# Cross scores in two steps with a shared bias product, and a planned order with a pause before each buffer's next use and longer weight loads

## The chip, the cores and the metric

The kernel runs on one core of one Trainium2 chip, in one launch. The metric is the device time of one execution in microseconds (us), from the runs listed below; smaller is better. TensorE (PE in the profile, its weight loads PEld), VectorE (DVE), ScalarE (ACT), GpSimd (POOL) and SyncE (SP, which here issues all DMAs) each work through their own queue of instructions in the order in which the program holds them, and wait for each other by semaphores.

## The reference

A decoder block with three sublayers, each followed by a residual sum and a layer norm, on x of shape (4, 512, 128) in fp32.

```python
def attn(x, Wq, Wk, Wv, Wg, Wa, ba, Wo, gn_w, gn_b):         # 16 heads of 64
    q, k, v = silu(x @ Wq), silu(x @ Wk), x @ Wv
    cum = cumsum(-softplus(x @ Wa + ba))
    decay = exp(where(causal, cum[i] - cum[j], -inf))
    o = ((q @ k.T) * decay) @ v
    o = groupnorm_over_tokens_and_channels_of_a_head(o) * gn_w + gn_b
    return (o * sigmoid(x @ Wg)) @ Wo

def xattn(ctx, query, W1, b1, W2, b2, W3):                    # 32 keys per sample
    q, k = query @ W1.T + b1, ctx @ W2.T + b2
    return (softmax(q @ k.T / 32) @ ctx) @ W3.T

def ffn(x, ...):                                              # 6 layers
    for i in range(6):
        # 16 heads of 64, windows of 32 tokens that also see the window before
        q, k, v = split(shift_tokens(x) @ Wqkv[i])
        q, k = rotary(l2norm(q) * q_scale[i]), rotary(l2norm(k) * k_scale[i])
        x = softmax(mask(q @ k.T * 8)) @ v @ Wo[i] + x
        a, gate = split(layernorm(shift_tokens(x)) * g + b @ W1[i] + b1[i])
        x = (a * gelu(gate)) @ W2[i] + b2[i] + x
    return x

x = layernorm(x + attn(x, ...))
x = layernorm(x + xattn(ctx, x, ...))
x = layernorm(x + ffn(x, ...))
```

## The kernel before

**Stages.** The front (class `Front`) does the first attention sample by sample, eight pairs of heads for each (`pair`), then the norm (`finish`) and the cross attention (`cross`). The layers (class `Layers`) work in units: layer, sample, half of the heads, token tile, 6 x 4 x 2 x 4 = 192 units. A unit projects q and k (three fp32r products each, lines 87 to 89, the `pq` and `pk` tiles), squares and rotates them (ACT line 1258, DVE lines 1242 and 1251, POOL line 1264), scales them by the inverse norm (POOL line 1362), transposes both (line 96, `ptq` and `ptk`), makes the window scores `s` (lines 1408 and 1421, 72 products on 64x32 tiles of the array, called S in the plan), the softmax (DVE 1441 and 1450, ACT 1460 and 1463, DVE 1466 and 1467, POOL 1473), transposes the result (line 1483, `pp`, then ACT 1487) and multiplies it by the values into `O` (line 1499, 64 products on 128x32 tiles). The values of two tiles are projected together and moved into window order by eight pairs of DMAs (`vb<-v`, lines 1313 to 1325). After the two halves of a sample its attention is added (`add_attention`), and the feed-forward part follows (`ffn`).

**Cross scores.** `cross` folds W1, W2 and the biases into a matrix M and a row br (made once in `setup_b`). For each sample it multiplies four token tiles by M (128 rows in the array) and adds br by a product with one row in the array, tile after tile, in one planned step:

```python
for t in range(NT):
    nc.tensor.matmul(view()[:, t, :], lhsT=x[:, tslice(t)], rhs=M[:, keys], start=True, stop=False)
    nc.tensor.matmul(view()[:, t, :], lhsT=unit, rhs=br[:, keys], start=False, stop=True)
```

An fp32 product of this kind is two passes, hence x2 for each in the profile.

**What sets the order.** Nothing is issued as it is written. Each step is recorded by `do` with its engine, a cost, what it reads and writes, and a priority: the number of its unit or pair plus an offset from the table `SHIFT`, by the step's name (group letter and running number). `Plan.order` then plays the steps through in the plan's own clock and writes down the order in which they start; that order is the program, on every engine. In it an engine takes the ready step of lowest priority number. On TensorE it may take another one whose priority is up to `KEEP` larger, if a change of kind costs less: `TURNS` and `TURN` hold what the plan charges for a change between kinds (`t` transposes, `S`, `O`, `f` the last product of the feed-forward part, `None` the projections). A step that writes a buffer starts only if one of that sort is free (`ROOM`: 3 + 2 + 2 + 1 banks of PSUM, 2 raw buffers for weights, and so on), and a buffer is counted free at the moment when its last user's planned cost has passed. `LAG` is what lies between a step's end and the start of another that needs it, `DMA` the same for loads of weights. The figures in these tables are the plan's own, not measurements.

**Loads of weights.** `load_half` and `load_values` load through the two raw buffers: `w0` and `w3` are the loads of Wq and Wk (lines 1067), `w6` of Wo (line 1086), `w7` of Wv (line 1089, tiles `wv00r` for layer 0 and half 0, `wv01r` for half 1), whose transposes `wvt` and products `wvo` (line 1100) fold Wv with Wo. `load_ffn` loads W1 (`w1r`, line 1157) and folds the bias (`pb`, line 1162). All are issued by SP, in the planned order, and the first layer's wait for the last sample's fifth pair of heads.

Of the kernel before, what the change touches and what calls it, by code (L numbers as in the profile page):

```python
# [20 lines left out]
B, S, D = 4, 512, 128  # L21
NT = S // P
H, DH = 16, 64
SK = 32
# [10 lines left out]
def tslice(t):  # L35
    return slice(t * P, (t + 1) * P)
# [97 lines left out]
class Plan:  # L134
# [5 lines left out]

    LAG = 0.25

    TURN = 0.04
    TURNS = {
# [3 lines left out]
    }  # L148

    KEEP = 4.5  # L150

    def __init__(self, room):
        self.room, self.steps, self.last = dict(room), [], {}
# [26 lines left out]
    def order(self):  # L180
        free, left, need, ready, after = dict(self.room), {}, {}, {}, {}
# [13 lines left out]
        waiting, busy, out, events, kinds = {}, set(), [], [], {}  # L195
# [24 lines left out]
        now = 0.0  # L220
        while events:
            now = events[0][0]
            while events and events[0][0] <= now + 1e-9:
                _, _, over, st = heapq.heappop(events)
                if not over:
                    heapq.heappush(waiting.setdefault(st.eng, []), (st.prio, st.n, st))
                    continue
                busy.discard(st.eng)
                for s in st.slots:
                    left[s] -= 1  # L230
                    if left[s] == 0 and s.tags:
                        free[s.got] += 1
            for eng, q in waiting.items():
                if eng in busy:
                    continue
                passed, pick, best = [], None, 0.0
                while q:
                    it = heapq.heappop(q)
                    if pick is not None and it[0] > least + self.KEEP:
                        passed.append(it)  # L240
                        break
                    took = room(it[2])
                    if took is None:
                        passed.append(it)
                        continue
                    give(took)
                    turn = self.turn(eng, kinds.get(eng), it[2].kind)
                    if pick is None:
                        least = it[0]
                    elif turn >= best:  # L250
                        passed.append(it)
                        continue
                    else:
                        passed.append(pick)
                    pick, best = it, turn
                    if turn == 0.0:
                        break
                for it in passed:
                    heapq.heappush(q, it)
                if pick is None:  # L260
                    continue
                st = pick[2]
                took = room(st)
                for s, g in took.items():
                    s.got = g
                busy.add(eng)
                st.start = now
                out.append(st)
                cost = st.cost + best
                kinds[eng] = st.kind  # L270
                heapq.heappush(events, (now + cost, st.n, 1, st))
                for nx, d in after.get(st, ()):
                    need[nx] -= 1
                    ready[nx] = max(ready[nx], now if d is None else now + cost + d)
                    if need[nx] == 0:
                        heapq.heappush(events, (ready[nx], nx.n, 0, nx))
# [5 lines left out]
class Work:  # L282
# [5 lines left out]
        t1=8, t2=4, sq=2, nx=2, n2=3, r=4, u=2, v=2, qT=2, kT=3, pr=3, mx=3, su=3, pT=2, vb=2,  # L288
# [3 lines left out]
    )  # L292

    SHIFT = dict(
        C1=5.5, C2=8.5, C3=-2.75, D0=19.5, D2=12.75, D3=-11.25, D4=-0.5, D6=3.25, D7=12.25, D8=-1.25, D9=-7.75,
        D10=-7.25, I0=-0.5, I2=1.25, N0=1, N1=21.5, N2=0.5, N3=-14.75, N4=-22, N5=-27, N6=5.25, O0=-0.25,
        O1=-17.25, O2=-10.5, O4=-0.25, P0=-3.75, P1=14.25, P2=19.75, P3=-2.75, P4=13, P5=8.5, P8=-9.5, P9=-3.5,
        P10=-1, P11=125.75, P12=-12.5, P13=-2.25, P14=4, P15=4.5, P16=-4.5, P17=0.25, P18=42.75, P19=-0.25,
        P20=11.5, P21=40.5, P22=-0.75, P23=-26.75, P24=-1.25, P25=-0.25, P26=-3, P27=-0.75, P28=-7.5, P29=-0.75,
        P30=0.25, P31=18.5, P32=52.25, P33=-1.5, P34=3.75, P35=-24, P36=11.5, P37=-8.25, P38=7.75, P39=6, S0=-2,  # L300
        S1=18.25, S2=18, S3=24.75, S4=4.75, S5=3, S7=33.5, S8=-2, V0=-0.25, V1=48.5, V2=-82.5, V3=-19, V4=-27.25,
        V5=-11, V6=1.5, V7=19.25, W0=13.5, W1=-1.5, W2=-4, W3=21, W4=-4.5, W5=-2, W6=2, W7=-6.25, W8=-0.25,
        W9=-0.25, W10=4, W11=0.75, X1=28.25, X2=-0.5, X3=-1.75, X4=-2, X5=42.25, X6=3.25, X7=1.25, X8=127.5,
        X9=24.75, X10=-7.25, X11=0.25, X12=-0.5, X13=-6.75, X14=-4.75, X15=-11, X16=4.5, X17=-0.5, a0=-0.25,
        a1=-0.25, a2=4.25, a3=4.25, f0=-22.25, f1=-1.75, f2=54.25, f3=-5, f4=-30, f5=-5.5, f6=-5, f7=-9.25,
        f8=-26.25, f9=7.5, f10=1, f11=0.25, f12=-37.5, f13=-6.75, f14=-13.75, f15=-6.5, f16=0.5, f17=-46.5,
        f18=4.25, f19=-14.75, f20=8, f21=3.25, f22=-30.25, f23=8.5, f24=-6.5, f25=-39.75, f26=81.5, f27=5.25,
        f28=-61.75, f29=12.5, g0=-15.5, g1=1.25, g2=5.75, g3=0.75, g4=-1.5, g5=7.25, g6=-1.75, k0=-1.75, k2=-1.5,
        k3=12, k4=2, k5=-16, k6=17.5, k7=2, p0=33.5, p1=10.25, q0=2.25, q1=-2.25, q2=-10.25, q3=-4.75, q4=-0.25,
        q5=1.75, q6=0.75, q7=-16.25, q8=-23, q9=-9, q10=-2.75, q11=-6.75, q12=-1.25, q13=-22.5, t0=7.25,  # L310
        t1=-31.75, t2=-1, t3=-3.25, t4=-29, t5=-6.75, t6=6.75, u1=7.25, u2=2.25, u3=2.25, u4=-20.75, u6=-1.5,
        u7=2.25, u8=3.25, u9=-12.25, u10=-7.25, u11=40.25, u12=31.25, u13=-2, u14=-1.75, u15=-23.75, u16=9,
        u17=0.5, u18=-7.75, u19=1.25, u20=9.5, u21=34.75, u23=-12, u24=-59.75, u25=-14.5, u26=-23, u27=-53.5,
        u28=-45.5, u29=-49.75, u30=-29, u31=-36.25, u32=-58, v0=6.75, v1=-0.5, v2=2, v4=0.5, v5=5.25, v6=-2.75,
        w0=-19, w1=2, w2=-4, w3=-58.25, w4=35.5, w5=-17.75, w6=-3, w7=2.75, w8=3.25, w9=-1, w10=1.5, w11=-10,
        w12=-6, w13=-4.75, w14=2.5, w15=-1.75,
    )

    PE3, PE_T, PE_S, PE_AV = 0.73, 0.37, 0.72, 1.01
    SPD = 0.62  # L320
    A512, V512 = 0.49, 0.61
    G_ADD, G_MUL, G16 = 1.25, 1.01, 0.23
    DMA = 8.0

    def __init__(self, k, plan):
        self.k, self.plan = k, plan
# [1 line left out]
    def do(self, eng, cost, fn, r=(), w=(), off=0.0, **kw):  # L328
        name = f"{self.group}{self.count}"
        self.count += 1  # L330
        self.plan.step(eng, cost, fn, r, w, prio=self.base + off + self.SHIFT.get(name, 0.0), **kw).name = name
# [73 lines left out]
class Front(Work):  # L405
# [571 lines left out]
    def cross(self, b):  # L977
        k, nc, do = self.k, self.k.nc, self.do
        M, br, cw, unit = self.bw
# [4 lines left out]
        pq = self.bank("mm", "pq" + nm)  # L984
        view = lambda: pq()[:, 0 : NT * SK].rearrange("p (t k) -> p t k", t=NT)

        def scores():
            for t in range(NT):
                nc.tensor.matmul(view()[:, t, :], lhsT=x[:, tslice(t)], rhs=M[:, keys], start=True, stop=False)
                nc.tensor.matmul(view()[:, t, :], lhsT=unit, rhs=br[:, keys], start=False, stop=True)  # L990

        do("PE", 2.7, scores, [X, bs], [pq], kind="g")
        sm = self.slot("bs", [P, 2, NT], "bs" + nm)
        e = self.slot("be", [P, NT, SK], "e" + nm)
        wide = lambda j: sm()[:, j].unsqueeze(2).to_broadcast([P, NT, SK])
# [36 lines left out]
class Layers(Work):  # L1032
# [47 lines left out]
    def load_values(self, W, l, h2):  # L1080
# [13 lines left out]
        for e in range(2):  # L1094
            rows = slice(e * 64, e * 64 + 64)
            ps = self.bank("mm", f"wvo{nm}{e}")

            def prod(ps=ps, rows=rows):
                for p in range(4):
                    nc.tensor.matmul(  # L1100
                        ps()[:, tslice(p)], lhsT=wt()[rows, tslice(p)], rhs=wo()[rows, p, :], start=True, stop=True
                    )

            self.do("PE", 0.85, prod, [wt, wo], [ps])
            self.do("ACT", self.A512, lambda ps=ps, e=e: nc.scalar.copy(hi()[:, e], ps()), [ps], [hi])
            self.do(
                "DVE",
                self.V512,
                lambda ps=ps, e=e: nc.vector.tensor_tensor(out=lo()[:, e], in0=ps(), in1=hi()[:, e], op=ALU.subtract),
                [ps, hi],  # L1110
                [lo],
            )
# [708 lines left out]
```

## Time and profile before

| | us |
|---|---|
| median of 3 runs | 2003.3 (2001.99 to 2007.96) |
| profiled execution, device time | 2008.77 |
| its span, first to last instruction | 2007.1 |
| busy: TensorE | 1850.5 (92%) |
| busy: VectorE | 1611.1 (80%) |
| busy: ScalarE | 1587.4 (79%) |
| busy: GpSimd | 1441.8 (72%) |
| mean granted TensorE clock | 0.976 of full |

The busy time is the union of an engine's instructions in one profiled execution. Matmuls are pipelined, so that the length of one product is more than it adds; what a group of products adds is read from the end of the group before to its own end. Idle time is put down to what ended it; "issue" means that nothing that the profile shows was waited for. The slices of the page are 50.2 us each. The front fills the first 360 us or so, then six layers of about 260 us each, which overlap at their borders.

### The profile page before, as it was taken

How to read it: one execution, taken by the hardware profiler on the slowest of the kernel's cores; microseconds unless marked ns; L12 is line 12 of the kernel's file. 1: busy time of each engine (PE TensorE's matmuls, PEld its weight loads, DVE VectorE, ACT ScalarE, POOL GpSimd, SP SyncE). 2: the span in 40 equal slices, each digit the busy share in tenths (PEclk: the TensorE clock that was granted, in tenths of full speed). 3: DMA queues.
4: the chain of work that ended last, by engine and by line, in shares of the span. 5: the costliest groups of instructions: out<-in, count | busy, mean ns of one | idle time of the engine just before them, and what ended most of it. 6: DMA issues, size and time to landing. Idle time of an engine off the chain costs nothing.

```text
span 2007.1 us, 71083 instructions
## 1 busy us (share of the span) xinstructions
PE 1850.5 (92%) x28633; PEld 1405.3 (70%) x28633; DVE 1611.1 (80%) x3482; ACT 1587.4 (79%) x4048; POOL 1441.8 (72%) x1847
## 2 busy tenths in 40 slices
PE   7999999788898999989999999999999998999996
PEld 5676677566676777767777777777777776767675
DVE  5787786757787798886998868989788897888885
ACT  7877765689887788878888888888878897788785
POOL 3444444666777688886887878878878888787882
PEclk9999997789999999999999999999999999999999
DMA  3000001254555565665555555656655565545662
GB/s 90 1 6 2 1 2 34 67 130 109 133 148 123 131 152 139 156 150 147 133 132 146 146 146 142 166 123 160 150 142 144 125 157 149 142 107 134 146 172 60
DMA packets 146464, 233.02 MB, mean 116 GB/s; under 512 B 23770, under 2 KB 39000, under 8 KB 146136
## 3 DMA queue, kind: packets, MB, share of 16 engines
q1 hardware_dynamic: 146136, 228.46, 45.7%
q8 instruction: 228, 3.74, 0.8%
q14 instruction: 100, 0.82, 0.1%
HBM read 31.25 MB, written 2.10 MB: 17 GB/s over the span
## 4 chain that ended last, share of the span: by engine, by line
PE 57%; ACT 18%; DVE 14%; DMA 4%; issue 3%; SPq 3%; POOL 1%; DVEq 0%; ACTq 0%; POOLq 0%
PE O L1499 6%; PE s L1421 4%; PE pv L87 4%; DMA vb<-v 4%; PE pv L89 3%; PE pv L88 3%; PE ptk L96 3%; PE pp L1483 3%; PE ptq L96 2%; SPq L1325 2%; PE pyf L1625 2%; DVE nx L1275 2%; ACT sq L1258 2%; ACT v L1306 2%; PE pq L87 1%
## 5 line engine op out<-in xcount | busy, mean ns | idle before, releaser
L1264 POOL TENSOR_TENSOR t1q<-t1q,t2q 128x512 f32<-128x512 f32 x192 | 248.7, 1295 | 66.4 <-DVE t2q L1251 62.6
L1264 POOL TENSOR_TENSOR t1k<-t1k,t2k 128x512 f32<-128x512 f32 x192 | 251.3, 1310 | 55.4 <-DVE t2k L1251 40.7
L1473 POOL TENSOR_TENSOR pr<-pr,su 128x512 f32<-128x512 f32 x192 | 204.2, 1068 | 91.0 <-DVE su L1467 73.7
L1306 ACT COPY v<-pv 128x512 f32<-128x512 f32 x384 | 219.8, 602 | 42.7 <-PE pv L89 37.4
L1275 DVE TENSOR_REDUCE nx<-sq 128x16 f32<-128x1024 f32 x192 | 231.8, 1207 | 4.9 <-ACT sq L1258 3.7
L1499 PE MATMUL O<-vb,pT 128*32 128x128 f32 x6144 | 210.9, 279 | 10.5 <-DMA vb<-v 4.8
L1499 PEld LDWEIGHTS O<-vb,pT 128*32 128x32 f32 x6144 | 165.0, 111 | 63.3 <-issue 30.3
L1362 POOL TENSOR_TENSOR t1q<-t1q,r 128x512 f32<-128x512 f32 x192 | 201.2, 1051 | 2.7
L1362 POOL TENSOR_TENSOR t1k<-t1k,r 128x512 f32<-128x512 f32 x192 | 200.9, 1049 | 0.0
L1421 PE MATMUL s<-kT,qT 64*32 64x64 f32 x12288 | 169.8, 223 | 22.6 <-issue 22.5
L1460 ACT ACTIVATE pr<-s,mx 128x64 f32<-128x64 f32 x768 | 178.2, 325 | 9.8 <-DVE mx L1441 9.8
L1441 DVE TENSOR_REDUCE mx<-s 128x4 f32<-128x256 f32 x384 | 145.6, 413 | 42.7 <-PE s L1421 41.3
L1242 DVE TENSOR_TENSOR t1k<-pk,tl 128x512 f32<-128x512 f32 x192 | 130.7, 681 | 56.0 <-PE pk L89 34.8
L1242 DVE TENSOR_TENSOR t1q<-pq,tl 128x512 f32<-128x512 f32 x192 | 130.7, 681 | 50.7 <-PE pq L89 37.0
L1421 PEld LDWEIGHTS s<-kT,qT 64*32 64x32 f32 x12288 | 151.0, 105 | 25.0 <-issue 24.5
L1258 ACT ACTIVATE sq<-pk 128x512 f32<-128x512 f32 x192 | 116.1, 610 | 41.6 <-DVE t1k L1242 23.9
L1251 DVE TENSOR_TENSOR t2q<-pq,tl 128x512 f32<-128x512 f32 x192 | 130.0, 677 | 21.0 <-ACT sq L1258 20.1
L1466 DVE TENSOR_REDUCE su<-pr 128x8 f32<-128x512 f32 x192 | 129.3, 673 | 20.8 <-ACT pr L1463 12.0
L1251 DVE TENSOR_TENSOR t2k<-pk,tl 128x512 f32<-128x512 f32 x192 | 130.4, 679 | 18.8 <-ACT sq L1258 18.6
L1487 ACT COPY pT<-pp 128x512 f32<-128x512 f32 x192 | 113.3, 596 | 24.3 <-PE pp L1483 23.1
L1258 ACT ACTIVATE sq<-pq 128x512 f32<-128x512 f32 x192 | 115.6, 614 | 20.9 <-DVE t1q L1242 18.2
L96 PE MATMUL ptq<-ident,t1q 128*128 128x128 f32 x768 | 120.0, 280 | 11.6 <-DVE t2k L1251 4.6
(1002 smaller groups left out, 5428.3 us busy)
## 6 DMA issues: line engine op xcount, KB each, us to landing
vb<-v SPq DMA_DIRECT2D x576, 256.0 KB
vb<-v SPq DMA_DIRECT2D x192, 128.0 KB
vb<-v SPq DMA_DIRECT2D x288, 64.0 KB
vb<-in_c_zero_dram SPq DMA_DIRECT2D x96, 64.0 KB
wo<-in_L_ffn_Wo_dram SPq DMA_DIRECT2D x12, 256.0 KB
tb<-in_c_tabs_dram SPq DMA_DIRECT2D x12, 256.0 KB
w1r<-in_L_ffn_W_dram SPq DMA_DIRECT2D x6, 341.0 KB
xt<-in_x_dram SPq DMA_DIRECT2D x4, 256.0 KB
```

Source lines behind the costliest of these rows:

```text
L96: self.nc.tensor.transpose(bank[: blk.shape[1], tslice(t)], blk, self.ident)
L1242: nc.vector.tensor_tensor(out=t1(), in0=ps().rearrange("p (h d) -> p h d", d=DH), in1=tl()[:, 2 * j, t : t + 1, :].to_broadcast([P, 8, DH] ...
L1251: nc.vector.tensor_tensor(out=t2().rearrange("p h (z d) -> p h z d", z=2), in0=ps().rearrange("p (h z d) -> p h z d", d=32, z=2)[:, :, ::- ...
L1258: do("ACT", self.A512, lambda ps=ps, j=j: nc.scalar.activation(sq()[:, j], ps(), AF.Square), [ps], [sq])
L1264: lambda t1=t1, t2=t2: nc.gpsimd.tensor_tensor(out=t1(), in0=t1(), in1=t2(), op=ALU.add),
L1275: nc.vector.tensor_reduce(out=near()[:, :, 0], in_=sq().rearrange("p j (h d) -> p (j h) d", d=DH), op=ALU.add, axis=AX.X,)
L1306: do("ACT", self.A512, lambda pv=pv, j=j, e=e: nc.scalar.copy(v()[:, j, e], pv()), [pv], [v])
L1362: lambda x=x, j=j: nc.gpsimd.tensor_tensor(out=x(), in0=x(), in1=r()[:, j].unsqueeze(2).to_broadcast([P, 8, DH]), op=ALU.mult),
L1421: nc.tensor.matmul(sv[e]()[rows, p, :], lhsT=qT()[c, p, rows], rhs=kT()[c, p, 32 * w : 32 * w + 64], start=False, stop=True, skip_group_ch ...
L1460: nc.scalar.activation(pr()[:, a, 1], sv[1]()[:, a], AF.Exp, bias=mx()[:, a, 1:2])
L1473: lambda: nc.gpsimd.tensor_tensor(out=flat(), in0=flat(), in1=su().unsqueeze(2).to_broadcast([P, 8, 64]), op=ALU.mult),
L1499: nc.tensor.matmul(o[rows, t], lhsT=pT()[:, p, rows], rhs=vb()[:, t % 2, w, tslice(p)], start=(h2 == t == p == 0), stop=(h2 == 1 and p == ...
```

## The change

The cross scores become two steps of two token tiles. In each, one bias product (one row in the array, 64 columns) opens both tiles' accumulation, and the two products with M follow. In the plan, a freed buffer is given back `GIVE` = 0.2 after its last user's end instead of at once; `DMA` goes from 8 to 11; `TURNS`, `KEEP` and four costs of TensorE steps have other values, the product of Wv with Wo (`prod`) costs 1.05 instead of 0.85, and the whole table `SHIFT` is another one, so that the order differs on all five engines. No other instruction is added or taken away.

```diff
+    GIVE = 0.2
+
     TURN = 0.04
     TURNS = {
-        ("t", "t"): 0.08, ("t", None): 0.0, (None, "t"): 0.0, ("t", "S"): 0.17, ("t", "O"): 0.17, (None, "S"): 0.09,
-        (None, "O"): 0.09, ("S", "t"): 0.17, ("S", None): 0.17, ("S", "O"): 0.27, ("S", "f"): 0.17,
-        ("O", "t"): 0.0, ("O", None): 0.0, ("O", "S"): 0.0, ("O", "f"): 0.0, ("t", "f"): 0.08,
+        ("t", "t"): 0.08, ("t", None): 0.0, (None, "t"): 0.06, ("t", "S"): 0.17, ("t", "O"): 0.17, (None, "S"): 0.12,
+        (None, "O"): 0.12, ("S", "t"): 0.2, ("S", None): 0.19, ("S", "O"): 0.19, ("S", "f"): 0.17,
+        ("O", "t"): 0.1, ("O", None): 0.1, ("O", "S"): 0.09, ("O", "f"): 0.1, ("t", "f"): 0.08, ("f", "O"): 0.2,
     }
 
-    KEEP = 4.5
+    KEEP = 6.5
...
+                if over == 2:
+                    for g in st.freed:
+                        free[g] += 1
+                    continue
                 busy.discard(st.eng)
+                st.freed = []
                 for s in st.slots:
                     left[s] -= 1
                     if left[s] == 0 and s.tags:
-                        free[s.got] += 1
+                        st.freed.append(s.got)
+                if st.freed:
+                    heapq.heappush(events, (now + self.GIVE, st.n, 2, st))
...
     SHIFT = dict(
-        C1=5.5, C2=8.5, C3=-2.75, D0=19.5, D2=12.75, D3=-11.25, D4=-0.5, D6=3.25, D7=12.25, D8=-1.25, D9=-7.75,
+        C0=4, C1=-17.5, C2=6.75, C3=4.75, D0=6, D2=40.75, D3=4.25, D4=-2.75, D5=3.5, D6=18.5, D7=24, D8=-6.25,
...
-    PE3, PE_T, PE_S, PE_AV = 0.73, 0.37, 0.72, 1.01
+    PE3, PE_T, PE_S, PE_AV = 0.72, 0.36, 0.7, 0.91
...
-    DMA = 8.0
+    DMA = 11.0
...
-        def scores():
-            for t in range(NT):
-                nc.tensor.matmul(view()[:, t, :], lhsT=x[:, tslice(t)], rhs=M[:, keys], start=True, stop=False)
-                nc.tensor.matmul(view()[:, t, :], lhsT=unit, rhs=br[:, keys], start=False, stop=True)
-
-        do("PE", 2.7, scores, [X, bs], [pq], kind="g")
+        def scores(t):
+            two = br[:, keys].unsqueeze(1).to_broadcast([1, 2, SK])
+            nc.tensor.matmul(view()[:, t : t + 2, :], lhsT=unit, rhs=two, start=True, stop=False, skip_group_check=True)
+            for j in range(t, t + 2):
+                nc.tensor.matmul(
+                    view()[:, j, :], lhsT=x[:, tslice(j)], rhs=M[:, keys], start=False, stop=True, skip_group_check=True
+                )
+
+        for t in (0, 2):
+            do("PE", 0.9, lambda t=t: scores(t), [X, bs], [pq], kind="g")
...
-            self.do("PE", 0.85, prod, [wt, wo], [ps])
+            self.do("PE", 1.05, prod, [wt, wo], [ps])
```

More of the change, by code (lines that the diff above doesn't have):

```diff
@@ L294 @@
     SHIFT = dict(
-        C1=5.5, C2=8.5, C3=-2.75, D0=19.5, D2=12.75, D3=-11.25, D4=-0.5, D6=3.25, D7=12.25, D8=-1.25, D9=-7.75,
[L296 to L314, printed above, removed]
@@ L315 @@
-        w0=-19, w1=2, w2=-4, w3=-58.25, w4=35.5, w5=-17.75, w6=-3, w7=2.75, w8=3.25, w9=-1, w10=1.5, w11=-10,
-        w12=-6, w13=-4.75, w14=2.5, w15=-1.75,
+        C0=4, C1=-17.5, C2=6.75, C3=4.75, D0=6, D2=40.75, D3=4.25, D4=-2.75, D5=3.5, D6=18.5, D7=24, D8=-6.25,
+        D9=-9, D10=-25, I0=0.5, I1=3.5, I2=9.75, N0=15.75, N1=21.75, N2=-5.25, N4=-10.25, N5=-24, N6=1, O0=1.25,
+        O1=7, O2=6.5, O3=9.75, O4=3.5, O5=-11.75, P0=-4, P1=20, P2=21.75, P3=-3, P4=15.25, P5=3.25, P6=-2,
+        P7=-1.25, P8=-0.75, P9=-3.5, P10=8.5, P11=137, P12=1.75, P13=-1.75, P14=15.75, P15=-11.75, P16=10,
@@ new lines @@
+        P17=-0.25, P18=72.25, P19=-1, P20=18.5, P21=66.25, P23=-1, P25=-0.25, P26=7.5, P27=-18.25, P28=-27,
+        P29=10.75, P31=23, P32=18.5, P33=-1.5, P34=-10.25, P35=-39.75, P36=15.5, P37=-16.5, P38=0.5, P39=7.25,
+        S0=-0.5, S1=13.5, S2=-0.25, S3=-7.5, S4=2, S5=-6, S6=-3.25, S7=60.5, S8=2.5, V1=51.25, V2=-102.5, V3=1,
+        V4=-18.75, V5=-25, V7=34.5, W0=9.75, W1=4.75, W2=-9.5, W3=23.75, W4=0.25, W5=-14, W6=15, W7=2, W8=-8.25,
+        W9=-4.25, W10=-11.25, W11=-2.75, X0=2.75, X1=43.75, X2=-4, X3=-5.75, X4=5, X5=66, X6=5, X7=-12.25,
@@ new lines @@
+        X8=128.25, X9=26, X10=-9, X11=3.5, X12=1, X13=-0.25, X14=-2, X15=1, X16=-5.75, X17=-11.75, X18=0.25,
+        a0=-13.5, a1=-26.25, a2=-1, a3=5.75, f0=-31, f2=57.5, f4=-43, f5=-12, f6=7.75, f7=-11.5, f8=-1.75,
+        f9=6.75, f10=-15.25, f11=-7.25, f12=-8.75, f13=-16, f15=-4.25, f16=-5, f17=-61.25, f18=-0.5, f19=3.75,
+        f20=11.5, f21=1.5, f22=2.25, f23=6.75, f24=9.5, f25=3.25, f28=11, f29=3, g0=-3.5, g1=2, g2=18.25,
+        g3=-7.25, g4=-13, g5=8.25, g6=-11, g7=3, k1=-0.5, k2=1.25, k3=8.25, k4=1, k5=-45.5, k6=3.5, k7=-0.5,
@@ new lines @@
+        p0=34.75, p1=23.5, q0=2.25, q1=-14.25, q2=-19.75, q3=-3, q4=1.5, q5=4, q7=-21.5, q8=-25.5, q9=-1.5,
+        q10=-20, q11=-22.5, q12=0.25, q13=1.75, t0=-17, t1=-37.5, t3=4.25, t4=-39.25, t6=-4, u1=7.75, u2=2.5,
+        u3=2.25, u4=-32.5, u6=-0.5, u7=2.5, u8=3.25, u9=-25, u10=-5.25, u11=37, u12=14.75, u13=-5.25, u14=3,
+        u16=11.25, u17=-2.5, u18=0.75, u19=-0.75, u20=10, u21=40.75, u22=2.75, u23=-25.25, u24=-62.75, u25=-36.5,
+        u26=-19.25, u27=-62, u28=-39, u29=-52.5, u30=-27.25, u31=-44.25, u32=-47.75, v0=-2.25, v1=-1, v2=7,
@@ L317 @@
+        v3=9.25, v4=-1.25, v5=-1.5, v6=7.5, w0=-33.5, w1=-9, w2=-21.25, w3=-58, w4=26.5, w5=-17.25, w6=-2,
+        w8=4.5, w10=-0.25, w11=-1.75, w12=1, w13=-26, w14=3, w15=-2.25,
     )
-    PE3, PE_T, PE_S, PE_AV = 0.73, 0.37, 0.72, 1.01
+    PE3, PE_T, PE_S, PE_AV = 0.72, 0.36, 0.7, 0.91
     SPD = 0.62
```

## Prediction

> **What bounds the kernel now.** I read the page first (busy shares, then the 40 slices), then busy time by stretch, then TensorE's order of time around the cross scores and in a middle layer, and last the waits of the DMA queue at the change from front to layers.
>
> ```profile
> PE 1850.5 (92%) x28633; PEld 1405.3 (70%) x28633; DVE 1611.1 (80%) x3482; ACT 1587.4 (79%) x4048; POOL 1441.8 (72%) x1847
> PEclk9999997789999999999999999999999999999999
> ```
>
> TensorE is the bound, at 92%. Its granted clock is full except in slices 7 to 9 (301 to 452 us), where the layers begin. By stretch (columns: length, busy of PE, PEld, DVE, ACT and POOL with instructions, granted clock, DMA share, GB/s):
>
> ```profile
> 0.00:297.70 297.70, 275.21 (x2347) 201.46 (x2348) 220.84 (x576) 222.09 (x535) 133.23 (x160) 0.99 0.06 17
> 297.70:338.60 40.90, 40.48 (x232) 29.18 (x230) 26.45 (x86) 21.32 (x51) 15.62 (x19) 0.71 0.10 30
> 338.60:550.00 211.40, 174.16 (x2481) 132.99 (x2481) 155.73 (x341) 168.02 (x365) 143.04 (x182) 0.89 0.42 106
> 550.00:1950.00 1400.00, 1320.00 (x22916) 1011.16 (x22917) 1173.41 (x2384) 1142.70 (x3021) 1130.58 (x1461) 1.00 0.57 143
> 1950.00:2007.10 57.10, 40.69 (x679) 30.46 (x669) 34.69 (x97) 33.26 (x78) 19.30 (x27) 0.92 0.33 80
> ```
>
> TensorE's idle time is 22.5 us in the front, 37.2 where the layers start, 80.0 in the 1400 us of steady layers and 16.4 at the end. No instruction of the layers changes, so only three things can move: TensorE's own time per group (which group stands before it), its idle time, and its clock.
>
> **Cross scores.** The old step alternates 128-row products with 1-row bias products:
>
> ```profile
> 294.19 0.41 PE L989 MATMUL pqB<-bM,X 128*128 128x32 f32 x2
> 294.52 0.40 PE L990 MATMUL pqB<-bbr,bone 1*128 1x32 f32 x2
> 294.86 0.41 PE L989 MATMUL pqB<-bM,X 128*128 128x32 f32 x2
> ```
>
> Each pair of passes starts 0.335 us after the one before, so eight take 2.7 us per sample. Passes inside a pair start some 0.13 us apart and end 0.11 apart: it is the change of kind that costs. A new step has one bias pair (0.34), one token pair after a change (0.34) and one without a change (0.22): 0.9 us, 1.8 for two. Saved: 4 samples x 0.9 = 3.6 us. The second step is entered and left once more, 0.2 us by the next rows, so 4 x 0.2 = 0.8 comes back. **-2.8 us.**
>
> **The clock after the cross scores.** The same view by stretch, cut where the clock changes:
>
> ```profile
> 294.10:297.70 3.60, 3.60 (x23) 3.14 (x23) 2.84 (x11) 1.91 (x6) 2.31 (x4) 1.00 0.00 0
> 297.70:314.80 17.10, 17.10 (x80) 12.28 (x78) 6.28 (x18) 5.84 (x14) 2.53 (x2) 0.50 0.13 39
> 331.80:338.60 6.80, 6.80 (x20) 4.52 (x18) 4.96 (x15) 2.57 (x5) 4.13 (x5) 0.50 0.26 77
> 430.80:434.20 3.40, 3.40 (x39) 2.38 (x37) 2.93 (x6) 1.63 (x3) 3.40 (x4) 0.50 0.01 2
> ```
>
> The cross scores run at 294.2, 299.0, 328.7 and 427.3 us, and each time that they fill a stretch of about 3.4 us the clock is halved right after it, although TensorE was busy throughout. Halved time behind them is 17.1 + 6.8 + 3.4 = 27.3 us, all of it full of work, so at most 13.7 us are lost. In the built order of the changed kernel the two halves of a sample lie some 8 to 21 us of TensorE's work apart, 0.9 us each, so no stretch is filled. The gain is between 0 (something else halves the clock) and 13.7; I take **-10**, near the upper end, as three of four places show the pattern.
>
> The Trainium skill ("TensorE: Matmul & The Clock Gate", Part 1, The HAM clock gate) speaks against this term: it says that an idle window of about 3.4 us throttles the clock and that busy time keeps it. By that rule busy scores cost no clock, the term is 0 and the sum -10 instead of -20. The rows show 3.60 us busy of 3.60 before the drop, so I follow the rows.
>
> **The order on TensorE.** The weights of the planner (TURNS, KEEP, SHIFT, the costs) only show as an order, which I compared group by group in the two built programs. What a change of kind costs stands in a middle layer:
>
> ```profile
> 1137.07 0.40 PE L89 MATMUL pq<-wq21h,yl 128*128 128x512 f32 x1
> 1137.30 0.60 PE L96 MATMUL ptk<-ident,t1k 128*128 128x128 f32 x4
> 1137.83 0.30 PE L1408 MATMUL s<-msk,identb 64*32 64x256 bf16 x8
> 1137.95 0.84 PE L1421 MATMUL s<-kT,qT 64*32 64x64 f32 x64
> ...
> 1139.28 0.39 PE L89 MATMUL pk<-wk21h,yl 128*128 128x512 f32 x1
> ```
>
> From end to end (start plus length), the transposes after a projection take 0.43, the scores S after them 0.89, the projection after S 0.88. After transposes a projection takes 0.69 to 0.71 and after S transposes take 0.58, so returning from small tiles costs 0.2 and 0.15. Over all pairs of groups in the trace, O takes 1.01 after another kind and 0.87 after O, and S costs 0.1 more after another kind where nothing stalls. In the new order 28 more projections follow small tiles (152 to 180: +5.6), 25 more three-block transposes of the front (4 to 29: +3.8), 20 fewer four-block ones (163 to 143: -3.0), 20 more O enter from another kind (+2.7) and 20 more S (+1.9). **+11 us.** The changed kernel switches more, not less. Least is 0, if they fall into idle time.
>
> Against it stand the S groups that run into each other:
>
> ```profile
> 1263.89 1.95 PE L1499 MATMUL O<-vb,pT 128*32 128x128 f32 x64
> 1265.78 0.30 PE L1408 MATMUL s<-msk,identb 64*32 64x256 bf16 x8
> 1265.90 0.75 PE L1421 MATMUL s<-kT,qT 64*32 64x64 f32 x55
> 1267.50 0.26 PE L1421 MATMUL s<-kT,qT 64*32 64x64 f32 x5 [0.85 <-issue]
> ...
> 1267.66 0.91 PE L1421 MATMUL s<-kT,qT 64*32 64x64 f32 x62
> ```
>
> Two S take 2.73 us here instead of 1.78, with 0.85 waited on nothing but TensorE's own issue. The mean over the 49 S that follow S is 1.34, 0.45 above one that stands alone; O after S is 0.31 dearer. S after S falls from 49 to 29, O after S rises from 16 to 25: -9.0 + 2.8, **-6** (ends: 0, and -16 at 0.85 each).
>
> **Loads of weights.** The plan now reckons 11 instead of 8 for them. In the profile they are slower than 8: wv00r is issued at 359.73 and its transposes start at 371.14.
>
> ```profile
> SPq L1157 <- POOL wq01l L1072: 8.1, 1, 8.1
> SPq L1089 <- PE wvo L1100: 6.7, 1, 6.7
> ```
>
> SP stands in order: the first layer's w1r waits 8.1 us for a raw buffer, and behind it wv01r waits for the next, so it is issued at 376.23 and its transposes start at 392.2, after 2.9 us of wait. In the new order wv01r stands ahead of w1r and takes the earlier buffer, some 8 us sooner; w1r then comes later, and its fold has 14 us of TensorE's work ahead of it instead of 19, still over the 11.4 measured. The first load's 2.8 us stay. Behind SP's entries the vb copies queue, which start after both. **-4**, between -15 (under half of the 37.2 us) and +8 (a fold that waits). In later layers the wv loads have 10 to 12 us of cover before and 11 to 19 after, and wait little now: nothing.
>
> **Delay for a buffer's next use.** The plan now frees a buffer 0.2 later. Counted over the 1,794 groups between 550 and 1950 us, 108 waited 0.1 to 0.3 us, 21 us together; these are what such a delay can fill with other work. Longer waits (113 us over 0.3) it can move either way. I take under half of the 21, **-8**; ends -30 (a third of the 80 and some) and +30 (next part).
>
> Cost figures of the plan alone (prod, PE3 and so on) move nothing beyond the order. Sum: -2.8 - 10 + 11 - 6 - 4 - 8 = -20. The profiled execution takes 2008.8 us (span 2007.1), 0.3% above the median of 2003.3; it becomes 1989, and the median 1983. A measurement can tell about 0.3%, 6 us.
>
> **Rivals.** *Slower by the softmax chain.* From S to the transposes pp of the same unit the new order leaves 6.6 us of TensorE's work in the median instead of 7.2. The chain itself (two maxima, the exponentials, the sum, POOL's product) ends 6.8 us after S in the median. Now pp waits 5 us in all, since real time from S to pp is 7.9. If two in five of the 192 units lose the whole 0.6, that is 46 us; without the -8 the rest is -12, so +34, 2037; it turns the sign from about one unit in ten. Against it: chain and cover have shortened together before, since part of the 6.8 is queueing. With fewer units hit, 2010 to 2025. 25%.
> *Nothing to see.* Something else in the front halves the clock as before, and delay and loads bring nothing: -2.8 + 11 - 6 = +2, 2005. 11%.
> *A larger gain.* A third of the steady idle time goes (27 us) and 12 of the start: -2.8 - 10 + 11 - 6 - 12 - 27 = -47, 1956. For it: the plan's figures for S, O and loads are nearer to the rows above; against: the more switches. 17%.
> *The forecast,* 47%.
>
> **How the numbers follow.** Faster is 0.64 (forecast and larger gain), same 0.11, slower 0.25. The forecast's own ends are some 1968 to 1998. For 8 in 10 the range reaches to 1950 below and 2020 above, which leaves out the far half of the slower rival and the tail of the larger gain.
>
> **What would show it.** Right: the cross scores at 0.9 us in two places, full clock between 290 and 340 us, wv01r issued before w1r, fewer S with waits on issue, TensorE's busy time hardly lower although idle time falls below 80 in the steady layers. Wrong: the clock halved in the same places (then -10 goes), pp waiting more than 20 us for POOL (the slower rival), or idle time in the steady layers above 90 us.

## The result, and the profile after

The changed kernel takes 2035.84 us (median of 4 runs, 2030.44 to 2038.97) where the kernel before takes 2005.63 in the runs beside it: a ratio of 1.0144, with a 95% interval of 1.0108 to 1.018. It is 30 us slower by the medians (29 by the ratio), not 20 us faster, and lies above the predicted range. The profiled execution took 2038.97 us, with a span of 2037.2 and a mean granted clock of 0.968 (0.976 before).

The page of the changed kernel, busy times and granted clock by slice:

```profile
PE 1860.3 (91%) x28617; PEld 1414.3 (69%) x28617; DVE 1616.1 (79%) x3482; ACT 1584.6 (78%) x4046; POOL 1438.3 (71%) x1847
PEclk9898998788999999999999999999999999999998
```

Busy time in two of the stretches, with the same cuts and columns as before:

```profile
297.70:338.60 40.90, 38.82 (x362) 29.14 (x363) 36.99 (x104) 25.88 (x63) 21.78 (x25) 0.96 0.09 27
550.00:1950.00 1400.00, 1301.35 (x22332) 994.51 (x22334) 1145.56 (x2324) 1117.68 (x2954) 1105.59 (x1424) 0.99 0.59 140
```

Three things stand there. The slow stretch at 297.7 us now has a clock of 0.96 instead of 0.71, as forecast. But slices 2 and 4, in the front, have lost clock that they had. And TensorE's idle time in the 1400 us of steady layers has grown from 80.0 to 98.7 us, which the prediction had named as a sign that it is wrong.

The loss is made in the layers: the last product of a sample's feed-forward part, followed through five successive layers, comes at 821, 1082, 1342, 1600 and 1852 us before, and at 804, 1062, 1334, 1605 and 1874 after. The changed kernel is 17 us ahead at the first of these marks and 20 at the second; over the next three intervals it loses 12, 13 and 16 us. Its waits have a line that the kernel before does not have at all (engine, tile and line, what it waited for: total us, times, longest):

```profile
ACT v L1318 <- DMA vb<-v: 18.0, 7, 4.4
```

ScalarE's copy of the projected values into `v`, of which there are two buffers, waits for DMAs that still read the older `v`. Four of the seven waits are long (3.0 to 4.4 us), near 759, 1087, 1358 and 1630 us. The interval between the first two marks holds none of them, and each of the three that lose holds one. ScalarE in order of time around the second:

```profile
1082.46 0.64 ACT L1499 COPY pT<-pp 128x512 f32<-128x512 f32 x1
1087.41 0.58 ACT L1318 COPY v<-pv 128x512 f32<-128x512 f32 x1 [4.30 <-DMA vb<-v]
```

And TensorE, which finds no free bank until that copy has been made:

```profile
1085.43 0.60 PE L1495 MATMUL pp<-ident,pr 128*128 128x128 f32 x4
1089.22 0.80 PE L87 MATMUL pk<-wk21h,yh 128*128 128x512 f32 x1 [3.18 <-ACT v L1318]
```

The stretch after it, by the same columns as above:

```profile
1083.30:1088.50 5.20, 2.44 (x42) 1.67 (x40) 2.75 (x6) 1.09 (x3) 2.06 (x4) 1.00 0.81 186
1088.50:1095.30 6.80, 6.08 (x48) 4.87 (x49) 2.69 (x4) 4.90 (x12) 4.57 (x4) 0.50 0.05 12
```

A wait of 4.3 us on ScalarE idles TensorE for 3.18 us, and then the clock is halved for 6.8 us that are 6.08 us full of work, so that some 3 us more are lost. By this estimate such a place costs about 6 us.

Why only the changed order has them is seen on SyncE. Its rows around this place, before and after; L1317 before and L1329 after are the same step, which moves the rows that lie between a pair's two tiles (`between` in the code, `q13` in the table of shifts):

```profile
1070.46 0.78 SPq L1313 DMA_DIRECT2D vb<-in_c_zero_dram  x2
1071.34 1.21 SPq L1317 DMA_DIRECT2D vb<-v  x2
1072.64 7.04 SPq L1325 DMA_DIRECT2D vb<-v  x6
```

```profile
1076.94 5.12 SPq L1337 DMA_DIRECT2D vb<-v  x6
1082.12 2.09 SPq L1329 DMA_DIRECT2D vb<-v  x2
```

Before, this step stands ahead of the six DMAs of its own pair, second of the pair's moves. After, it is the last, and here it stands even behind six DMAs (three steps) of the next pair, which take 5.12 us to issue; the plan reckons 0.62 for each DMA, 3.7 for the six. So the older `v` stays in use some 5 us longer. The page of the changed kernel adds how long such a DMA (64 KB) takes from issue to landing, in the median of 288, the last column:

```profile
vb<-v SPq DMA_DIRECT2D x288, 64.0 KB, 2.6
```

The plan does not see this. It counts `v` free when the planned cost of the SyncE step that issues the DMAs has passed, and with `GIVE` 0.2 later, while the landing comes 2.6 us after the issue.

### The profile page after: what moved, and what is told of

It is laid out like the page before. It is cut to its first block, busy times and chain, and to the rows that moved or that the text cites. A ratio compares the mean times of both kernels' runs of the same rounds, so it can differ in the third digit from the quotient of the medians.

```text
span 2037.2 us, 70854 instructions
## 1 busy us (share of the span) xinstructions
PE 1860.3 (91%) x28617; PEld 1414.3 (69%) x28617; DVE 1616.1 (79%) x3482; ACT 1584.6 (78%) x4046; POOL 1438.3 (71%) x1847
## 4 chain that ended last, share of the span: by engine, by line
PE 51%; ACT 19%; DVE 18%; issue 4%; DMA 3%; SPq 2%; POOL 2%; ACTq 0%; DVEq 0%; POOLq 0%
PE O L1511 7%; PE s L1433 4%; DMA vb<-v 3%; PE pv L87 3%; ACT sq L1270 3%; PE pyf L1637 3%; PE pp L1495 2%; PE ptk L96 2%; PE pv L89 2%; PE pv L88 2%; DVE nx L1287 2%; PE ptq L96 2%; ACT v L1318 2%; ACT pr L1472 2%; DVE t1k L1254 2%
## 5 line engine op out<-in xcount | busy, mean ns | idle before, releaser
L1511 PE MATMUL O<-vb,pT 128*32 128x128 f32 x6144 | 221.2, 281 | 13.9 <-ACT pT L1499 10.1
L1511 PEld LDWEIGHTS O<-vb,pT 128*32 128x32 f32 x6144 | 169.1, 112 | 68.8 <-ACT pT L1499 21.3
L1397 ACT COPY kT<-ptk 128x512 f32<-128x512 f32 x192 | 115.2, 607 | 33.0 <-PE ptk L96 32.3
```

The source lines that it names most:

```text
L1511: nc.tensor.matmul(o[rows, t], lhsT=pT()[:, p, rows], rhs=vb()[:, t % 2, w, tslice(p)], start=(h2 == t == p == 0), stop=(h2 == 1 and p == ...
```

## Experiments

Theory V: the loss is these waits. Theory S: it is the softmax chain, the slower rival of the prediction. Theory W: it is the more frequent changes of kind on TensorE. The kernel before was run again beside each group of experiments, and each ratio is to those runs. Where a code cut is shortened, `...` marks it.

**A third buffer for `v`.** The changed kernel's order is untouched; the third buffer lies where constants of the front were, and the raw tiles are 682 instead of 768 wide.

```diff
...
+            self.nv += 1
+            if self.nv > 12 and self.nv % 3 == 0:
+                return k.vx.rearrange("p (j e n) -> p j e n", j=2, e=2)
+            return pooled()
...
```

> The changed kernel in its own order, with a third buffer for the projected values v (the plan still reckons with two; room for it by placing the front's constants in it, which are done with by then). In the changed kernel ACT waits 18 us in 7 stretches for DMAs vb<-v before it may write v, which the kernel before never does, and TensorE waits 14.7 us behind those copies. If these waits are the main cause: 12 to 16 us less than the changed kernel, about 2020. If the softmax chain or the extra changes of kind are: within 4 us of the changed kernel, 2032 to 2040.

Measured: 2006.13 us, ratio 0.9993 (0.9972 to 1.0014). All of the loss is gone, 30 us and not the 12 to 16 that were expected: the wait's own length is not all that it costs. Its waits and its steady stretch:

```profile
ACT v L1329 <- DMA vb<-v: 3.7, 1, 3.7
```

```profile
550.00:1950.00 1400.00, 1317.09 (x22902) 1007.71 (x22901) 1169.30 (x2382) 1138.20 (x3011) 1127.25 (x1455) 0.99 0.61 142
```

Idle time in the steady layers falls from 98.7 to 82.9 us. Theory S's sign is the wait of the transposes `pp` (matmuls and weight loads) for the softmax's last product `pr`: 2.9 us before, 11.0 after and still 8.2 here. The order on TensorE, and with it the changes of kind, is that of the changed kernel. So neither S nor W carries the loss.

**The control: the same buffer in the kernel before.** The same edit, in the order of the kernel before.

> The order of the kernel before, unchanged, with the third buffer for v put where the front's constants were. Theory V (the loss is ScalarE's copies into v that wait for the DMAs that still read the older v, and only the changed order makes them wait): the kernel before has no such wait, so a third buffer buys it nothing; 2000 to 2011 us, a ratio of 0.997 to 1.003. Rival theory M (a third buffer for v, or the other place in memory, helps any order by about what it helped the changed one, 30 us): 1970 to 1985 us.

Measured: 2008.22 us, ratio 0.9998 (0.9978 to 1.0019). The buffer helps only the order that waits for it.

**Half of the dose.** The third buffer serves the first three layers only; against the edit above:

```diff
-            if self.nv > 12 and self.nv % 3 == 0:
+            if 12 < self.nv <= 48 and self.nv % 3 == 0:
```

> The changed kernel's order, with the third buffer for v used in layers 0 to 2 alone, so that ScalarE's long waits near 759 and 1087 us can go and those near 1358 and 1630 us stay. Theory V with the price by stall (about 30 us for four long stalls, 7 us each, of which 4 are the wait and the rest the lower clock behind it): 2018 to 2024 us. Rival theory F (the first stall throws the later stages out of step, and the rest follows from that): with the first two gone nearly all of it comes back, 2004 to 2012 us. Rival theory L (only the late ones count, since the early loss is made up before the end): 2028 to 2038 us.

Measured: 2016.98 us, ratio 1.0068 (1.0039 to 1.0096), 1 us below what V expected and between the two rivals' numbers. The two long waits of the later layers have stayed (3.93 and 4.25 us), and the earlier ones are gone.

```profile
ACT v L1329 <- DMA vb<-v: 10.3, 5, 4.2
```

**The one step on SyncE.** With two buffers again, the step is put right behind its pair's other moves.

```diff
-            for st in plan.order():
+            order, own = plan.order(), {}
+            for st in list(order):
+                if st.eng == "SP" and st.name in ("q9", "q10", "q11", "q12"):
+                    own[st.n - int(st.name[1:])] = st
+                elif st.name == "q13" and st.n - 13 in own:
+                    order.remove(st)
+                    order.insert(order.index(own[st.n - 13]) + 1, st)
+            for st in order:
```

> The changed kernel with two buffers for v and its order untouched on TensorE, ScalarE, VectorE and GpSimd. On SyncE alone, the step that moves the rows between a pair's two tiles (line 1329 of the changed kernel) goes right behind the pair's other moves wherever the changed order put it later: 11 of 96 such steps move, by one to three places, three of them from behind three moves of the next pair (1083, 1354 and 1624 us). Theory V with that step as the cause: ScalarE's waits near 1087, 1358 and 1630 us go or shrink to 1 us, the one near 759 stays, ScalarE's waits for these DMAs fall from 18 to 5 or 8 us, and the time by about twice that: 2008 to 2017 us. Rival (the DMAs as a whole are late at these places, not this one): the waits stay over 14 us and the time at 2027 to 2038 us.

Measured: 2012.35 us, ratio 1.0038 (1.0005 to 1.007). Moving 11 steps of one queue takes back 21 of the 29 us (1.06 of 1.44%). Its profiled execution was the longest of its ten runs (2019.96), so only its waits are read:

```profile
ACT v L1318 <- DMA vb<-v: 6.1, 6, 3.3
```

The long waits near 1087, 1358 and 1630 us are gone, and the one near 759 us (3.25 us), where another step is the last to read the older `v`, has stayed, as expected.

**The counter-test.** In the kernel before, the same step is put late at three places.

```diff
...
+            for n, m in ((5104, 5210), (6547, 6653), (7990, 8096)):
+                order.remove(at[n])
+                order.insert(order.index(at[m]) + 1, at[n])
...
```

> The counter-test: the kernel before, with the same step put late at three places on SyncE (near 1056, 1316 and 1573 us), behind three moves of the next pair, as the changed kernel has it; nothing else is moved. Theory V: ScalarE's copies into v, which come at 1074.5, 1334.6 and 1592.1 us, then wait 4 to 6 us each, 12 to 18 in sum where there are none, and the time grows by twice that: 2025 to 2040 us. Rival (the changed order as a whole is what costs, and such a wait is made up for): under 2015 us.

Measured: 2038.78 us, ratio 1.0172 (1.0121 to 1.0222), within what was expected, but with waits that were longer, so that each microsecond of wait cost less than the two reckoned. Two of its three long waits follow the sum:

```profile
ACT v L1306 <- DMA vb<-v: 26.3, 5, 9.0
```

```profile
1079.30 0.58 ACT L1306 COPY v<-pv 128x512 f32<-128x512 f32 x1 [8.97 <-DMA vb<-v]
1350.73 0.58 ACT L1306 COPY v<-pv 128x512 f32<-128x512 f32 x1 [7.70 <-DMA vb<-v]
```

Three steps moved on SyncE make the kernel before as slow as the changed one, with TensorE's order untouched. Put together, for the two orders that this document starts from:

| kernel | ScalarE's waits for these DMAs, us | ratio to before |
|---|---|---|
| before | none | 1 |
| changed, third buffer | 3.7 | 0.9993 |
| changed, one step earlier | 6.1 | 1.0038 |
| changed, third buffer in three layers | 10.3 | 1.0068 |
| changed | 18.0 | 1.0144 |
| before, one step later | 26.3 | 1.0172 |

Against before, a microsecond of wait costs between 1.3 (34 us for 26.3) and 1.6 us (29 for 18.0); from the third buffer to the changed order it is 2.1 (30 for 14.3). What comes on top of the wait is in part the clock behind it: time at half the clock between 550 and 1950 us is 10 us before, 34 in the changed kernel and 17 with the third buffer. This part is loose: the last of the runs below (loads and products together), which has no such waits, has 27.

**The plan told of the landing.** The changed kernel is planned anew, with a buffer of `v` counted free only when the DMAs that read it have landed.

```diff
+        do("LAND", 0.01, lambda: None, ready[:1], [], hold=[last] if t else [])
+        do("LAND", 0.01, lambda: None, ready[1:], [], hold=[v])
```

> The changed kernel with two buffers for v, planned anew: the plan now counts a buffer of v free only when the DMAs that read it have landed. ScalarE's waits for those DMAs should be under 5 us in sum in place of 18 in any case. Theory V alone: the loss goes, 2004 to 2012 us. Rival theory T (the table of shifts suits only the plan that it was made with, as in the two runs with tables exchanged): the new order loses 3 to 4% whatever the waits for v do, 2060 to 2090 us.

Measured: 2063.75 us, ratio 1.0283 (1.025 to 1.0317). The waits are 2.5 us, as they should be, and yet it is slower: the rival T held. So waits for `v` explain the changed order's loss, and not the time of any order; what costs in this one is not separated by a run.

**The tables exchanged.** The changed kernel with the shifts of before, and the kernel before with the shifts of the changed one. The names of the steps behind the cross scores are moved by one, since these are one step in one kernel and two in the other. The first lines of the first edit:

```diff
     SHIFT = dict(
-        C0=4, C1=-17.5, C2=6.75, C3=4.75, D0=6, D2=40.75, D3=4.25, D4=-2.75, D5=3.5, D6=18.5, D7=24, D8=-6.25,
...
+        C1=5.5, C2=8.5, C3=-2.75, D0=19.5, D2=12.75, D3=-11.25, D4=-0.5, D6=3.25, D7=12.25, D8=-1.25, D9=-7.75,
...
```

> The changed kernel (two-step scores, GIVE, KEEP, TURNS, DMA and costs as changed) planned with the table SHIFT of before. If the plan's figures are what makes the order worse, whatever the table: 2030 or more. If the new table is to blame: 2000 to 2015. If a table only suits the figures that it was made with, it is slower than both, 2040 or more.

> The kernel before (one-step scores, no GIVE, its KEEP, TURNS, DMA and costs) planned with the table SHIFT of the changed kernel. If the new table is to blame: about as slow as the changed kernel, 2030 to 2040. If the plan's figures are to blame: 2000 to 2015. If a table only suits its own figures: slower than both, 2040 or more.

Measured: 2084.47 us, ratio 1.0379 (1.0337 to 1.042), and 2081.26 us, ratio 1.0369 (1.0321 to 1.0418): both slower than either kernel, as the third expectation of each has it. With the run above, three plans that differ from the one that their table was made with lose 2.8 to 3.8%. So the plan's figures and the table can't be judged one without the other, and what the single figures (`GIVE`, `DMA`, `KEEP`) are worth stays open.

**The cross scores alone.** The new products in the one planned step of the kernel before, whose order is otherwise untouched.

```diff
         def scores():
-            for t in range(NT):
...
+            for t in range(0, NT, 2):
+                two = br[:, keys].unsqueeze(1).to_broadcast([1, 2, SK])
...
         do("PE", 2.7, scores, [X, bs], [pq], kind="g")
```

> The kernel before, in its own order on every engine, with the new products of the cross scores (one bias product per two tiles) in the one planned step. My clock term: each sample's scores take 1.8 instead of 2.7 us, no stretch of 3.4 us is filled with them, so the halved clock behind them (27 us of it) goes: 10 to 13 us less with the 3.6 us of the scores themselves, 1990 to 1996. Rival (something else in the front halves the clock anyway): the scores' 3.6 us alone, 1999 to 2003.

Measured: 2004.69 us, ratio 0.9989 (0.9967 to 1.0011), above both expected ranges. In the profile both halves of the term are there, the products (two steps from 296.39 to 298.30 us, 1.9 instead of 2.7) and the clock:

```profile
296.39 0.43 PE L990 MATMUL pqB<-bbr,bone 1*128 1x64 f32 x2
...
297.67 0.63 PE L992 MATMUL pqB<-bM,X 128*128 128x32 f32 x4
```

```profile
297.70:338.60 40.90, 38.94 (x316) 28.05 (x315) 34.84 (x112) 25.75 (x59) 20.78 (x25) 1.00 0.11 31
```

That the old products bring the halving is seen in more than these two traces. In the four traces of the old order with the old products (before, its third buffer, its late step, its exchanged loads), the clock is halved three times each, near 300, 332 and 430 us, after 3.6 us with TensorE busy throughout. In the three traces of this order with the new products, alone or with another edit, it never is after such a stretch. But it is not the filling of 3.4 us that decides: in the first run with exchanged tables the new products stand back to back (259.11 to 261.02 us), and there the clock is halved too:

```profile
259.00:262.60 3.60, 3.60 (x33) 2.56 (x31) 2.72 (x6) 1.84 (x7) 1.18 (x1) 0.99 0.02 5
262.60:266.00 3.40, 3.40 (x18) 2.79 (x19) 2.25 (x8) 2.83 (x8) 1.34 (x2) 0.51 0.00 0
```

The first layer's marks come 14 to 22 us earlier, but those after 1340 us only 11, and the end 7 in this profile and 2 by the medians. **With the third buffer beside it** the question was whether waits for `v` had eaten the rest.

> The order of the kernel before with the new cross-score products in their one planned step, and the third buffer for v. If the first layer's gain of the products (marks 14 to 22 us earlier) was given back in waits for v, it now reaches the end: 1990 to 1997 us. If it was given back in other waits (TensorE's transposes waiting for VectorE, stretches at half the clock), the third buffer changes nothing beside the products alone: 2000 to 2010 us.

Measured: 2009.07 us, ratio 1.0003 (0.9981 to 1.0026). They had not; to what else the layers gave it back stays open.

**The loads.** In the kernel before, SyncE issues wv01r ahead of w1r.

```diff
...
+            w1, wv = (next(s for s in order if s.n == n) for n in (1585, 1568))
+            order.remove(wv)
+            order.insert(order.index(w1), wv)
...
```

> The order of the kernel before with one exchange: SyncE issues wv01r ahead of the first layer's w1r, as the changed kernel does. If the weights of the values are what TensorE waits for at the change from front to layers (its waits at the transposes of Wv and at the products with Wo are 11.9 us in the kernel before and 1.6 us in the changed one), those waits fall by some 3 to 10 us and the time by as much: 1995 to 2003 us, a ratio of 0.995 to 0.9985. Rival (something else is late next there, the fold of W1 among it, or the layers give it back): 2003 to 2008 us, a ratio of 0.999 to 1.001.

Measured: 2007.18 us, ratio 1.0000 (0.9979 to 1.0021): the rival holds. The load is issued at 366.65 instead of 376.23 us, and its transposes wait as before, first the kernel before and then this one:

```profile
392.23 0.66 PE L96 MATMUL wvt<-ident,wv01r 128*128 128x128 f32 x4 [2.66 <-ACT v L1306]
```

```profile
390.63 0.66 PE L96 MATMUL wvt<-ident,wv01r 128*128 128x128 f32 x4 [2.65 <-ACT v L1306]
```

The bracket says what they wait for: ScalarE's copy of `pv` into `v`, which frees a bank, and not the load. **Both together**, loads and products:

> The exchange of the two loads and the new cross-score products together, in the order of the kernel before. If the two gains add up (products 2 us or so by their own run, loads 4 to 10 us), 1992 to 2000 us, a ratio of 0.993 to 0.997. If what the start of the layers gains is given back in the layers whatever it comes from, 2001 to 2008 us.

Measured: 2005.87 us, ratio 0.9997 (0.9972 to 1.0022); nothing adds up. No version here is measurably faster than the kernel before.

## Why the prediction was wrong, point by point

- **The step that failed** is "The order on TensorE": I compared the new order group by group on TensorE only, and took the other engines' queues as followers. The loss sits in SyncE's queue: one step there, put late, makes ScalarE wait 18.0 us for buffers of `v`, where it waited for none. The built order showed it (the shift `q13=-22.5` becomes `q13=1.75`), and a planned step that only issues DMAs does not end when the plan thinks that it ends. This term, +29 us, was in neither the sum nor a rival, which is to say that it was put at nothing without a reason.
- **Slower by the softmax chain** had the right sign, and its 2037 us lies 1 us from the measured time, but by luck: the mechanism is wrong. The waits of `pp` for `pr` did rise, from 2.9 to 11.0 us, but 8.2 of them stay when the time has come back.
- **The clock after the cross scores (-10).** At its place the mechanism came as forecast: with fewer bias products the clock there is 1.00, though a filled stretch of 3.4 us is not its condition. As a gain it was mis-sized: the products and the clock together bring -2 us (at most 0.33%, 6.6 us, by the interval). In the changed kernel half the clock turns up elsewhere in the front (27 us of it in the first 340, 31 before). At 54 us, where TensorE was busy throughout before, it is idle for 1.67 of 3.70 us, and then the clock is halved:

```profile
54.00:57.70 3.70, 2.03 (x25) 1.67 (x22) 3.05 (x15) 3.69 (x13) 0.95 (x2) 1.00 0.00 0
57.70:67.90 10.20, 10.20 (x50) 6.86 (x50) 4.80 (x13) 8.53 (x24) 3.52 (x5) 0.50 0.01 2
```

  At the waits of the layers the Trainium skill ("TensorE: Matmul & The Clock Gate", Part 1, The HAM clock gate), which ties the lower clock to idle windows, roughly fits the rows: 3.18 us idle, then half the clock. At the cross scores of the kernel before it did not, with 3.60 us busy of 3.60, and the rows above have half the clock after an idle time of half that length.
- **Cross scores (-2.8).** 1.9 us for the two steps in the old order and 0.99 for each step in the changed kernel, instead of the 0.9 reckoned; right to 0.2 us per sample.
- **Changes of kind (+11).** Not seen. With the changed order and the third buffer TensorE is busy for 1844.8 us, against 1850.5 before, at the same mean clock of 0.976; the sum had +8 for scores and changes of kind together. Busy time is a union over pipelined products, so this does not price one change of kind.
- **Fewer S after S (-6).** The saving is not seen. The waits of S on TensorE's own issue became fewer, as forecast, but longer, here of the kernel before and of the changed one (25.4 us in 20 with the third buffer):

```profile
PE s L1421 <- issue: 22.5, 26, 2.3
```

```profile
PE s L1433 <- issue: 30.1, 20, 3.4
```

- **Loads of weights (-4).** Refuted in the kernel before, where an earlier load changes nothing (1.0000, within 0.2%). I had read the 2.9 us at wv01r's transposes as a wait for the load; the row names ScalarE.
- **Delay for a buffer's next use (-8).** Nothing of it is seen: with the third buffer TensorE is idle for 82.9 us in the steady layers, instead of 80.0. The delay was not tested alone. It is 0.2 us where the buffer that mattered needed the 2.6 us of a landing.

Together: with the waits for `v` taken away, the change as a whole is worth nothing that can be measured (0.9993), where the sum had -20. Most of the clock's -10, the delay's -8 and the -6 of S did not come. TensorE's waits at Wv's transposes and products do go in the changed order (from 6.3 us in three waits to none), but the earlier load alone does not bring that. With the third buffer the five marks come 25, 25, 22, 21 and 10 us before those of the kernel before, and the end 2 us before it: the start does gain, and the last layers give it back; no run shows why. With an interval of 4 us to either side the terms can't be told apart more finely. Of the signs named for being right, the scores at their length, the clock (0.96) and the earlier load all came; they were signs of the order, and not of the time.

## What to carry to other kernels

When an order changes, compare it on every queue, the one that issues DMAs first of all, and follow each small ring of buffers from its last reader to its next writer; where the last reader is a DMA, the buffer is free at its landing, behind whatever was put ahead of it in the queue. Read from the bracket what a stalled instruction waits for before pricing the removal of what looks late. A gain at the start of a long pipeline is not yet one at its end: here 14 to 22 us in the first layer became 2.

## What the runs showed of the hardware that was not expected

A wait can cost more than itself when it idles TensorE: 4.3 us on ScalarE led to 3.18 us of idle TensorE and then 6.8 us at half the clock. The clock was also halved with TensorE busy for 3.60 of the 3.60 us before. And less time at half the clock in the first 340 us (31 us before, 14 with the new products in the same order) bought hardly any time at the end: some 8 us of TensorE's work by half of the difference, an estimate, and 2 us by the medians.
